# Turning normed tokens and slot rows by VectorE and transfers instead of TensorE, and a fixed engine for one copy

## The chip, the cores and the metric

The kernel runs on one core of a Trainium2 chip. The metric is the device time of one execution in microseconds, the median of several runs; lower is better. Profiled executions come with a trace of each engine: PE (TensorE's products), PEld (its weight loads), DVE (VectorE), ACT (ScalarE), POOL (GpSimd), and SPq, the queue on which SyncE issues transfers.

## The reference, cut to what matters

Two batches of 1024 tokens of 256 features pass through four residual steps, everything in float32:

```
x = x + L0_xattn(layernorm(x), ctx)       # 8 heads, softmax over 16 keys of the window
x = x + L0_ffn(layernorm(x))              # 8 groups, no nonlinearity between its two products
x = x + L1_xattn(layernorm(x), ctx, ctx)  # 16 heads, sigmoid instead of softmax
x = x + L1_ffn(layernorm(x))              # a mixture with 1024 slots

def L1_ffn(x):
    xn = rms_norm(x, gamma_x)
    se = rms_norm(slot_embeds, gamma_slot)
    logits = einsum('bsd,etd->bset', xn, se)
    dispatch = softmax(logits, over the tokens)
    slots = einsum('bsd,bset->betd', xn, dispatch)
    processed = gelu(slots @ w1) @ w2
    combine = softmax(logits, over the slots)
    return einsum('bnd,bsn->bsd', processed, combine)
```

The last step takes the larger part of the time. Below it is called the mixture, and the third step layer 1.

## The kernel before, in words

**Tiling.** The 2048 tokens are four quads of four tiles of 128 tokens; `xq[q]` holds a quad, tokens on the partitions, and is updated in place by each residual step. TensorE contracts over the partitions, so whatever is to be contracted over its features has to be turned first: features on the partitions, tokens along the row. The kernel before does that on TensorE, with a product against the identity, into a PSUM bank, and copies the bank to SBUF.

**Stages.** (1) The first attention runs per quad as `weigh` and `attend`. `attend` (L756) turns the attention weights on TensorE, copies them to `atT` (L762) and multiplies them with the folded values (L767). (2) The first feed-forward network folds its two weights per group g into one matrix (`product`, L522), and its biases into one row (`bias_rows`, mostly on VectorE at L553, then `bias`, L559); `norm_ff` and `feed_forward` use them per quad. (3) Layer 1 takes the quads in turn (L950). For each half c of the heads it makes scores (psg, L957), a Tanh on ScalarE (sg, L966) and the weighted values (poT, L996), whose eviction writes `oT` (L1003). Between scores and weighted values other work is put: at c = 0 the output product of the quad before (pf, L911), at c = 1 the queries of the next quad (pq, L897). (4) The mixture: `norm_tokens` (L154), `turn_tokens` (L175) and `logits` (L184) per token tile, then dispatch, `gather`, `hidden`, `processed` and `combine`.

**What is turned where.** `layernorm` (L482) of layer 1 writes `hn` and turns it by `transposed` (L120, eight turns of 128x128 on TensorE per quad, line L125, pt_a for layer 1, pt_f for the feed-forward network). `turn_tokens` turns the mixture's tokens in the same way (L180). `norm_slots` (L820) scales the 1024 slot rows by their own factor (squares L826, scaling L834), and `turn_slot_rows` turns a quarter of them at a time on TensorE (L842) while its eviction (L843) multiplies by the two gammas, which by then lie along the partitions. One tensor is already turned without TensorE: the mixture's combine weights `ec`. `turn` (L228) transposes blocks of 32x32 on VectorE (L236) into `tr`, and 16 transfers from SBUF to SBUF (L243) then put the blocks in their places.

**What sets the order.** A scheduler reorders the instructions of each engine at build time by program order and its own estimate of readiness; each engine then runs its queue strictly in the written order, and so does SyncE with its transfers. From L1012 on, ScalarE's order is as in the program. Operations written as `nc.any` are given to ScalarE or VectorE by the scheduler. Pools limit how many tiles of a tag are alive (`bufs`): a writer waits until the last reader of the tile that it replaces is done. Quad 1's `hn` takes the buffer that quad 0's turns on TensorE have read.

Of the kernel before, what the change touches and what calls it, by code (L numbers as in the profile page):

```python
# [9 lines left out]
FP = mybir.dt.float32  # L10
# [40 lines left out]
def tile_kernel(  # L51
# [9 lines left out]
    bo0: bass.AP,  # L61
    wff_in: bass.AP,
    b2: bass.AP,
    gammas: bass.AP,
    w1_in: bass.AP,
    slots_in: bass.AP,
# [25 lines left out]
    nc.gpsimd.memset(m_half, -0.5)  # L92
    xq = [const.tile([P, QT, D], FP, name=f"x{q}") for q in range(NQ)]

    gxs = const.tile([P, 2, DC], FP, name="gxs")
    gx, gs = gxs[:, 0, :], gxs[:, 1, :]
    ggx = const.tile([P, DC], FP, name="ggx")

    parity = const.tile([P, 2], FP, name="parity")
    nc.vector.tensor_reduce(  # L100
# [2 lines left out]
        AX.XY,  # L103
        ALU.add,
    )
    seT = const.tile([P, DC, NSLOT], FP, tag="seT", name="seT")

    def moments(xt, name):

# [10 lines left out]
    def transposed(src, dst, name, side=0):  # L120

        for c in range(DC):
            pt = bank(f"pt_{name}_{c}", side)
            for t in range(QT):
                nc.tensor.transpose(pt[:, ts(t, P)], src[:, t, ts(c, P)], ident)  # L125
            nc.any.tensor_copy(dst[:, c, :], pt)


    outr = out.rearrange("(q t p) d -> q p t d", t=QT, p=P)
# [43 lines left out]
        xhs[q] = xh  # L173

    def turn_tokens(q):  # L175
        xhT = pools["mw"].tile([P, DC, QN], FP, tag="xhT", name=f"xhT_{q}", bufs=2)
        for c in range(DC):
            pt = bank(f"pt_m_{q}_{c}", 1)
            for t in range(QT):
                nc.tensor.transpose(pt[:, ts(t, P)], xhs[q][:, t, ts(c, P)], ident)  # L180
            copy(c, xhT[:, c, :], pt)
        xhTs[q] = xhT

    def logits(b, s):  # L184

        q, t = b * QB + s // QT, s % QT
        if s == 0:
            zcs[b] = stat.tile([P, ST], FP, tag="zc", name=f"zc_{b}")
            rmaxs[b] = pools["md"].tile([P, NSLOT], FP, tag="rmax", name=f"rmax_{b}")
        lg = keep[b].tile([P, NSLOT], FP, tag=f"lg_{s}", name=f"lg_{b}_{s}")  # L190
        lgs[b][s] = lg
        nm = stat.tile([P, 2], FP, tag="nm", name=f"nm_{b}_{s}")
        for n in range(NSLOT // 512):
            pl = bank(f"pl_{b}_{s}_{n}", 0)
            for dc in range(DC):
                nc.tensor.matmul(  # L196
                    pl,
                    lhsT=xhTs[q][:, dc, ts(t, P)],
                    rhs=seT[:, dc, ts(n, 512)],
                    start=(dc == 0),  # L200
                    stop=(dc == DC - 1),
                )

            nc.vector.tensor_tensor_reduce(  # L204
                lg[:, ts(n, 512)], pl, zero.to_broadcast([P, 512]), -1.0,
                BIG if n == 0 else nm[:, 0:1], ALU.add, ALU.min, nm[:, n : n + 1],
            )

            rm = rmaxs[b][:, ts(n, 512)]
            if s == 1:  # L210
                nc.vector.scalar_tensor_tensor(
                    rm, lgs[b][0][:, ts(n, 512)], -1.0, pl, ALU.mult, ALU.max
                )
            elif s > 1:
                nc.vector.tensor_tensor(rm, rm, pl, ALU.max)
        if t == 0:

            ecs[q] = keep[b].tile([P, 2, QT, 512], FP, name=f"ec_{q}")
        nc.scalar.activation(  # L219
            ecs[q][:, :, t, :],  # L220
            lg.rearrange("p (h n) -> p h n", h=2),
            AF.Exp,
            bias=nm[:, 1:2],
            scale=-1.0,
            accum_out=zcs[b][:, s : s + 1],
        )
# [241 lines left out]
    with (  # L468
# [4 lines left out]
        wk1s, wv1s, wq1s, wo1s = (w1s[:, i] for i in range(4))  # L473
        se = w1p.tile([P, EC, D], FP, name="se")

        NCT, NPE = DC * 2 * B * NK, DC * NK
        fr = w1p.tile([P, NCT + NPE + NG * OC], FP, name="fr")
        ctxd = fr[:, 0:NCT].rearrange("p (c b e s) -> p c b e s", c=DC, b=B, e=2)
# [3 lines left out]
        def layernorm(xt, name, side=0):  # L482
            mv, rstd = moments(xt, name)
            hn = lnp.tile([P, QT, D], FP, tag="hn", name=f"hn_{name}")
            for t in range(QT):
                nc.vector.tensor_scalar(  # L486
                    hn[:, t, :], xt[:, t, :], mv[:, t, 0:1], rstd[:, t : t + 1],
                    ALU.subtract, ALU.mult,
                )
            hT = lnp.tile([P, DC, QN], FP, tag="hT", name=f"hT_{name}")  # L490
            transposed(hn, hT, name, side)
            return hT

        wide = ExitStack()
# [96 lines left out]
        def load_layer1():  # L591
            nc.sync.dma_start(out=w1s, in_=w1_in)
            nc.sync.dma_start(out=se, in_=slots_in)
            nc.sync.dma_start(out=gxs, in_=gammas)

        with tc.tile_pool(name="p0", bufs=1) as p0, tc.tile_pool(name="a0", bufs=2) as a0:

# [158 lines left out]
            def attend(q):  # L756
# [2 lines left out]
                for t in range(QT):  # L759
                    nc.tensor.transpose(pat[:, ts(t, P)], atf[:, ts(t, P)], ident)  # L760
                atT = a0.tile([P, QN], FP, tag="atT", name=f"atT_{q}")
                nc.any.tensor_copy(atT, pat)  # L762
                for i in range(2):
                    po = bank(f"po0_{q}_{i}")
                    for k in range(2):
# [49 lines left out]
        with (  # L815
# [4 lines left out]
            def norm_slots():  # L820
# [9 lines left out]
                nc.vector.tensor_scalar(sn, sn, RMS_EPS, None, ALU.max)  # L830
                nc.vector.reciprocal(sn, sn)
                nc.vector.tensor_scalar(sn, sn, float(D) ** 0.5, None, ALU.mult)
                for c in range(EC):
                    nc.vector.tensor_scalar(  # L834
                        se[:, c, :], se[:, c, :], sn[:, c : c + 1], None, ALU.mult
                    )
                nc.vector.tensor_tensor(ggx, gx, gs, ALU.mult)

            def turn_slot_rows(dc, h):
                pt = bank(f"pse_{dc}_{h}", 1)  # L840
                for c in range(4):
                    nc.tensor.transpose(pt[:, ts(c, P)], se[:, 4 * h + c, ts(dc, P)], ident)  # L842
                nc.vector.tensor_scalar(  # L843
                    seT[:, dc, ts(h, 512)], pt, ggx[:, dc : dc + 1], None, ALU.mult
                )

# [82 lines left out]
            for c in range(C1):  # L931
# [12 lines left out]
                None,  # L944
                ALU.mult,
            )
            queries(0)
            bias(7)
            work = ExitStack()
            for q in range(NQ):  # L950
                b = q * QN // S
                oTs[q] = a1.tile([P, C1, QN], FP, tag="oT", name=f"oT_{q}")
                for c in range(C1):
# [15 lines left out]
                    if c == 0:  # L969
                        if q == 0:  # L970
# [4 lines left out]
                            pools["mw"] = work.enter_context(  # L975
                                tc.tile_pool(name="mw", bufs=1, reuse_waits="tile")
                            )
                            norm_slots()
                        if q + 1 < NQ:
                            hTs[q + 1] = layernorm(xq[q + 1], f"a1_{q + 1}", 1)  # L980
                        if q > 0:
                            output(q - 1, (0, 1) if q + 1 < NQ else (0,))
                            turn_slot_rows(*divmod(q - 1, 2))
                        if q + 1 == NQ:
                            turn_tokens(0)
                    elif q + 1 < NQ:
                        queries(q + 1)
                        if q + 2 == NQ:
                            norm_tokens(0)
                            turn_slot_rows(1, 1)  # L990
                    else:
                        output(q - 1, (1,))
                        logits(0, 0)
# [21 lines left out]
    for u in range(1, B * ST + 2):  # L1015
        b, s = divmod(u, ST)
        if b < B:
            if s % QT == 1:
                q = u // QT + 1
                if q < NQ:  # L1020
                    norm_tokens(q)
            logits(b, s)
            if s % QT == 2:
                q = u // QT + 1
                if q < NQ:
                    turn_tokens(q)
        v = u - ST
        if v == 1:
            nc.vector.reciprocal(zcs[0], zcs[0])
# [113 lines left out]
```

## Time and profile before

| | |
|---|---|
| median of 3 runs | 461.45 us (461.29 to 461.98) |
| the profiled execution | 461.42 us, of which the trace's span is 459.6 us |
| granted TensorE clock | 1.00 throughout |
| first products of stage 1 and 2 end, layer 1's loop begins | about 123 us |
| first logits of the mixture | 170.0 us |
| last logits, gather begins | about 236 us |
| hidden and output of batch 0, gather of batch 1 begins | 347 us |
| VectorE's busy time in 66 to 108 us | 38.1 of 42 us |
| VectorE's busy time in 120 to 180 us | 35.2 of 60 us |
| ScalarE's busy time in the same 60 us | 24.7 us |
| transfers issued between 81 and 241 us | none |

A profile's group line reads: line, engine, operation, destination <- sources, count, then busy time and mean nanoseconds of one. A line of the waits names who waited for whom, the sum in us, how often and the longest. A line of the chain of work that ended last, or of a timeline, gives start, duration and what ran. Matrix products in float32 are recorded twice per instruction, turns once.

### The profile page before, as it was taken

What the parts mean: (1) busy time and instruction counts of PE and PEld (TensorE: products, weight loads), DVE (VectorE), ACT (ScalarE), POOL (GpSimd) and SP (SyncE); (2) the same over time, 40 slices, a digit from 0 to 9 for tenths busy, and PEclk for the clock granted to TensorE, in tenths of its full rate; (3) what the DMA queues carried; (4) which work ended last, traced back from release to release, by engine and by line L of the source; (5) the groups of instructions that cost most, each with busy time, mean ns of one, the idle gap of its engine ahead of it and who ended that gap; (6) DMA issues with size and microseconds to landing.
All of it is one profiled execution on the core that took longest, in us unless ns stands there. A gap on an engine that the chain in (4) does not pass through costs nothing.

```text
span 459.6 us, 5446 instructions
## 1 busy us (share of the span) xinstructions
PE 446.4 (97%) x2032; PEld 322.2 (70%) x2032; DVE 261.1 (57%) x623; ACT 110.8 (24%) x205; POOL 84.9 (18%) x84
## 2 busy tenths in 40 slices
PE   6999897999999999999999999999999999999997
PEld 5788795888645555445458854688888874488886
DVE  0487889897256677987776279611331539911111
ACT  1212331211344441342573306300000003410000
POOL 3011332325111101100878910000000000000000
PEclk9999999999999999999999999999999999999999
DMA  8994691500000000000007534140252040430011
GB/s 287 411 429 198 260 427 45 185 0 1 1 1 0 2 0 1 0 0 1 0 1 227 89 52 72 33 80 0 52 98 36 12 79 1 82 102 1 11 47 35
DMA packets 74381, 38.61 MB, mean 84 GB/s; under 512 B 68465, under 2 KB 70641, under 8 KB 72945
## 3 DMA queue, kind: packets, MB, share of 16 engines
q1 hardware_dynamic: 74354, 38.26, 27.4%
q8 instruction: 16, 0.26, 0.2%
q14 instruction: 11, 0.09, 0.1%
HBM read 27.76 MB, written 2.10 MB: 65 GB/s over the span
## 4 chain that ended last, share of the span: by engine, by line
PE 82%; DVE 6%; POOL 1%; issue 0%
PE psl L289 12%; PE pc L455 12%; PE pp L430 12%; PE pl L196 11%; PE pmh L364 11%; PE pmt L522 6%; PE pq L897 3%; PE pf L911 3%; PE po L580 2%; PE psg L957 2%; PE poT L996 2%; DVE b2z L553 1%; DVE hn_f L486 1%; PE po L767 1%; PE pt_a L125 1%; PE pb L273 1%
## 5 line engine op out<-in xcount | busy, mean ns | idle before, releaser
L522 PE MATMUL pmt<-wg 128*128 128x256 f32 x256 | 60.1, 393 | 3.8 <-DMA wg<-in_wff_dram 3.8
L289 PE MATMUL psl<-xh,lg 128*128 128x258 f32 x256 | 58.7, 381 | 0.0
L522 PEld LDWEIGHTS pmt<-wg 128*128 128x128 f32 x256 | 49.9, 198 | 11.4 <-DMA wg<-in_wff_dram 4.3
L196 PE MATMUL pl<-seT,xhT 128*128 128x512 f32 x128 | 56.1, 592 | 0.0
L455 PE MATMUL pc<-pr,ec 128*128 128x256 f32 x256 | 55.6, 379 | 0.0
L430 PE MATMUL pp<-ms,mh 128*128 128x256 f32 x256 | 55.6, 379 | 0.0
L430 PEld LDWEIGHTS pp<-ms,mh 128*128 128x128 f32 x256 | 48.6, 190 | 7.5 <-DVE mh L408 0.5
L455 PEld LDWEIGHTS pc<-pr,ec 128*128 128x128 f32 x256 | 48.6, 190 | 6.6
L289 PEld LDWEIGHTS psl<-xh,lg 128*128 128x128 f32 x256 | 47.4, 190 | 7.2 <-issue 0.5
L196 PEld LDWEIGHTS pl<-seT,xhT 128*128 128x128 f32 x128 | 24.1, 190 | 27.9 <-issue 26.3
L278 POOL TENSOR_TENSOR lg<-lg,mb 128x1024 f32<-128x1024 f32 x16 | 37.2, 2366 | 32.3 <-ACT mb L150 27.9
L462 DVE SCALAR_TENSOR_TENSOR x<-pc,zc,x 128x256 f32<-128x256 f32 x16 | 7.7, 484 | 42.3 <-PE pc L455 42.3
L442 DVE COPY pr<-pp 128x512 f32<-128x512 f32 x8 | 5.5, 692 | 45.5 <-PE pp L430 45.5
L219 ACT ACTIVATE ec<-lg,nm 128x1024 f32<-128x1024 f32 x16 | 18.4, 1148 | 41.6 <-DVE nm L204 41.6
L398 ACT COPY mh<-pmh 128x512 f32<-128x512 f32 x8 | 4.6, 572 | 89.6 <-PE pmh L364 89.6
L374 ACT ACTIVATE mh<-mh 128x512 f32<-128x512 f32 x32 | 19.0, 626 | 21.1 <-DVE mh L408 16.1
L364 PE MATMUL pmh<-slT,ms 128*128 128x512 f32 x48 | 24.0, 592 | 0.0
L553 DVE SCALAR_TENSOR_TENSOR b2z<-wg,fr,b2z 128x256 f32<-128x256 f32 x48 | 23.6, 494 | 0.3
L297 DVE RECIPROCAL rz<-psl 128x1 f32<-128x1 f32 x16 | 2.6, 164 | 32.7 <-PE psl L289 32.7
L966 ACT ACTIVATE sg<-psg 128x512 f32<-128x512 f32 x32 | 16.5, 603 | 18.0 <-PE psg L957 18.0
L236 DVE STREAM_TRANSPOSE tr<-ec 128x512 f32<-128x512 f32 x32 | 20.1, 679 | 0.0
L281 ACT ACTIVATE lg<-lg 128x1024 f32<-128x1024 f32 x16 | 16.5, 1049 | 12.2 <-POOL lg L278 12.2
(169 smaller groups left out, 585.9 us busy)
## 6 DMA issues: line engine op xcount, KB each, us to landing
wg<-in_wff_dram SPq DMA_DIRECT2D x6, 2048.0 KB, 12.4
ec<-tr SPq DMA_DIRECT2D x128, 64.0 KB, 2.1
xT<-in_xT_dram SPq DMA_DIRECT2D x4, 512.0 KB, 13.4
x<-in_x_dram SPq DMA_DIRECT2D x4, 512.0 KB, 14.9
wg<-in_wff_dram SPq DMA_DIRECT2D x2, 1024.0 KB, 11.3
ms<-in_m_dram SPq DMA_DIRECT2D x1, 2048.0 KB, 8.3
out_dram<-x SPq DMA_DIRECT2D x16, 128.0 KB, 1.8
wg<-in_wff_dram SPq DMA_DIRECT2D x3, 512.0 KB, 6.0
```

What stands on the lines that cost most here:

```text
L196: nc.tensor.matmul(pl, lhsT=xhTs[q][:, dc, ts(t, P)], rhs=seT[:, dc, ts(n, 512)], start=(dc == 0), stop=(dc == DC - 1),)
L219: nc.scalar.activation(ecs[q][:, :, t, :], lg.rearrange("p (h n) -> p h n", h=2), AF.Exp, bias=nm[:, 1:2], scale=-1.0, accum_out=zcs[b][:, ...
L236: nc.vector.transpose(tr[:, :, :, t, :].rearrange("p r c n -> p c r n"), half[:, t, :].rearrange("p (c r n) -> p c r n", c=EC // 2, r=R4),)
L278: nc.gpsimd.tensor_tensor(lgs[b][s], lgs[b][s], mbs[b], ALU.add)
L281: nc.scalar.activation(lgs[b][s], lgs[b][s], AF.Exp, scale=-1.0)
L289: nc.tensor.matmul(pz[:, 0:XW], lhsT=lgs[b][s][:, ts(c, P)], rhs=xhs[b * QB + s // QT][:, s % QT, :], start=(s == 0), stop=(s == ST - 1),)
L364: nc.tensor.matmul(to, lhsT=lefts[i][:, ts(j, P)], rhs=slTs[b][:, i, 0:512] if i < 2 else rights[b][i], start=True, stop=True,)
L374: nc.scalar.activation(h, h, AF.Gelu)
L430: nc.tensor.matmul(pp[:, ts(k, D)], lhsT=hss[b, g, fc // 2][:, fc % 2, ts(2 * c2 + k, P)], rhs=m12s[1][:, fc, :], start=(fc == 0), stop=(f ...
L455: nc.tensor.matmul(pc[:, 0:D], lhsT=turned[:, c // 4, c % 4, t, :], rhs=prs[b, c // 4][:, c % 4, :], start=(c == 0), stop=(c == EC - 1),)
L522: nc.tensor.matmul(pm[:, ts(hc, D)], lhsT=w1g[:, oc, ts(hc, P)], rhs=w2g[:, oc, :], start=(oc == 0 and hc == 0), stop=(oc == OC - 1 and hc ...
L553: nc.vector.scalar_tensor_tensor(acc, weights[g][1][:, oc, :], b1s[:, g, oc : oc + 1], acc, ALU.mult, ALU.add)
```

## The change

Six things are done together.

1. A function `turned` does what `turn` does for `ec`, for a tile of four times 128x256: four block transposes on VectorE into `tr`, then 16 transfers on SyncE.
2. Layer 1's quads 1 to 3 (not quad 0), all four quads of the mixture's tokens, and the slot rows in two halves are turned by it. The feed-forward network's norms stay on TensorE.
3. The norms are written earlier: quad 1's before layer 1's first queries, quad q + 2's during quad q; the mixture's quads 0 and 1 during layer 1's quads 1 and 2, and quads 2 and 3 at the first and third token tile of the logits. `hT` and `xhT` get three buffers instead of two.
4. The gammas can no longer be applied while slot rows are evicted, as there is no eviction. Both are loaded as rows on all partitions, multiplied by GpSimd, and GpSimd multiplies the slot rows by them; the scaling by the rows' own factors goes from VectorE to ScalarE.
5. `seT` is laid out by halves of slots.
6. The copy of `atT` is fixed to ScalarE.

```
+    def turned(src, dst, tr):
+        for t in range(QT):
+            nc.vector.transpose(
+                tr[:, :, :, t, :].rearrange("p r c n -> p c r n"),
+                src[:, t, 0:D].rearrange("p (c r n) -> p c r n", c=DC, r=R4),
+            )
+        to = dst.rearrange("p c (t i n) -> p (c t) i n", t=QT, i=R4)
+        for i in range(R4):
+            for r in range(R4):
+                nc.sync.dma_start(
+                    out=to[ts(r, SQ), :, i, :],
+                    in_=tr[ts(i, SQ), r].rearrange("p c t n -> p (c t) n"),
+                )
...
     def turn_tokens(q):
-        xhT = pools["mw"].tile([P, DC, QN], FP, tag="xhT", name=f"xhT_{q}", bufs=2)
-        for c in range(DC):
-            pt = bank(f"pt_m_{q}_{c}", 1)
-            for t in range(QT):
-                nc.tensor.transpose(pt[:, ts(t, P)], xhs[q][:, t, ts(c, P)], ident)
-            copy(c, xhT[:, c, :], pt)
+        xhT = pools["mw"].tile([P, DC, QN], FP, tag="xhT", name=f"xhT_{q}", bufs=3)
+        tr = pools["mw"].tile([P, R4, DC, QT, SQ], FP, tag="tr", name=f"tr_m_{q}", bufs=2)
+        turned(xhs[q], xhT, tr)
...
-            hT = lnp.tile([P, DC, QN], FP, tag="hT", name=f"hT_{name}")
-            transposed(hn, hT, name, side)
+            hT = lnp.tile([P, DC, QN], FP, tag="hT", name=f"hT_{name}", bufs=3)
+            if side is None:
+                tr = lnp.tile([P, R4, DC, QT, SQ], FP, tag="tr", name=f"tr_{name}")
+                turned(hn, hT, tr)
+            else:
+                transposed(hn, hT, name, side)
...
-            nc.sync.dma_start(out=gxs, in_=gammas)
+            nc.sync.dma_start(out=gx, in_=gx_in)
+            nc.sync.dma_start(out=ggb, in_=gammas.partition_broadcast(P))
...
-                nc.any.tensor_copy(atT, pat)
+                nc.scalar.copy(atT, pat)
...
+                gg = ggb[:, 0, :]
+                nc.gpsimd.tensor_tensor(gg, gg, ggb[:, 1, :], ALU.mult)
                 for c in range(EC):
-                    nc.vector.tensor_scalar(
-                        se[:, c, :], se[:, c, :], sn[:, c : c + 1], None, ALU.mult
-                    )
-                nc.vector.tensor_tensor(ggx, gx, gs, ALU.mult)
+                    nc.scalar.activation(
+                        se[:, c, :], se[:, c, :], AF.Copy, scale=sn[:, c : c + 1]
+                    )
+                for h in range(2):
+                    sh = se[:, ts(h, QT), :]
+                    nc.gpsimd.tensor_tensor(
+                        sh, sh, gg.unsqueeze(1).to_broadcast([P, QT, D]), ALU.mult
+                    )
-            def turn_slot_rows(dc, h):
...
+            def turn_slot_rows(h):
+                tr = lnp.tile([P, R4, DC, QT, SQ], FP, tag="tr", name=f"tr_se_{h}")
+                turned(se[:, ts(h, QT), :], seT[:, h], tr)
...
+            hTs[1] = layernorm(xq[1], "a1_1", None)
             queries(0)
             bias(7)
+            norm_slots()
+            turn_slot_rows(0)
...
-                            norm_slots()
-                        if q + 1 < NQ:
-                            hTs[q + 1] = layernorm(xq[q + 1], f"a1_{q + 1}", 1)
+                        if q + 2 < NQ:
+                            hTs[q + 2] = layernorm(xq[q + 2], f"a1_{q + 2}", None)
                         if q > 0:
                             output(q - 1, (0, 1) if q + 1 < NQ else (0,))
-                            turn_slot_rows(*divmod(q - 1, 2))
-                        if q + 1 == NQ:
-                            turn_tokens(0)
                     elif q + 1 < NQ:
                         queries(q + 1)
-                        if q + 2 == NQ:
-                            norm_tokens(0)
-                            turn_slot_rows(1, 1)
+                        if 0 < q:
+                            norm_tokens(q - 1)
+                            turn_tokens(q - 1)
+                        if q == 0:
+                            turn_slot_rows(1)
...
-            if s % QT == 1:
-                q = u // QT + 1
-                if q < NQ:
-                    norm_tokens(q)
+            if u in (1, 3):
+                norm_tokens(QB + u // 2)
+                turn_tokens(QB + u // 2)
             logits(b, s)
-            if s % QT == 2:
-                q = u // QT + 1
-                if q < NQ:
-                    turn_tokens(q)
```

## The prediction

> **What bounds the kernel now.** I read the page's shares first, then TensorE's own waits, then the chain that ended last.
>
> ```profile
> PE 446.4 (97%) x2032; PEld 322.2 (70%) x2032; DVE 261.1 (57%) x623; ACT 110.8 (24%) x205; POOL 84.9 (18%) x84
> ```
>
> ```profile
> PE pmt L522 <- DMA wg<-in_wff_dram: 3.8, 1, 3.8
> PE po L767 <- DVE atT L762: 3.4, 1, 3.4
> PE pt_f L125 <- DVE e L741: 1.2, 1, 1.2
> PE pwk L686 <- ACT vblk L675: 1.0, 1, 1.0
> PE po L767 <- ACT atT L762: 0.7, 1, 0.7
> ```
>
> TensorE is the bound: 97% busy, and its waits sum to 10.1 us in 459.6. They all lie before 73 us; from there to the last product it never starves. So an instruction taken off TensorE after 73 us is worth its pitch on TensorE, if the data that it made still arrives in time. The chain gives the pitch (an instruction's mean of 270 ns overlaps its neighbours):
>
> ```profile
> 131.36 3.63 PE pq L897 x8
> 134.99 1.00 PE poT L996 x8
> 135.98 1.07 PE psg L957 x8
> 137.05 1.02 PE pt_a L125 x8
> 138.08 3.46 PE pf L911 x16
> 141.53 0.44 PE pse L842 x4
> 141.97 0.99 PE poT L996 x8
> 142.97 1.07 PE psg L957 x8
> ```
>
> Eight turns of normed tokens take 0.87 to 1.02 us, four turns of slot rows 0.44. One quad of layer 1 is pq to pq, 12.7 us.
>
> The other resource that matters is the sync queue, since the mixture's weights are already turned in the new way. The answer for the tile tr (minimum, median, maximum ns):
>
> ```profile
> L243 SPq DMA_DIRECT2D ec<-tr x128: 585/627/1613, 245.5 to 401.4; - x128
> L236 DVE STREAM_TRANSPOSE tr<-ec x32: 668/670/712, 242.5 to 390.7; 128x512 f32<-128x512 f32 x32
> DMA to landing us min/median/max: 2.1/2.1/5.0
> ```
>
> Sixteen transfers follow one another at 0.63 us though each lands 2.1 us later: the issue is what is serial. Between 81 and 241 us that queue issues nothing in this kernel.
>
> **What is removed.** Off TensorE go the turns of layer 1's quads 1 to 3 (0.87 + 1.02 + 1.02 = 2.9 us in the chain), of four slot-row parts (4 x 0.44 = 1.8) and of four mixture quads (4 x 0.87 = 3.5): 72 turns, **8.2 us**. All lie after 110 us, where TensorE is the bound.
>
> **The copy of atT.** VectorE's timeline in the one attend that waits:
>
> ```profile
> 70.35 1.00 DVE L553 SCALAR_TENSOR_TENSOR b2z<-wg,fr,b2z 128x256 f32<-128x256 f32 x2
> 71.26 0.15 DVE L837 TENSOR_TENSOR ggx<-gxs 128x2 f32<-128x2 f32 x1
> 71.33 0.68 DVE L739 TENSOR_REDUCE mx<-psc 128x32 f32<-128x512 f32 x1
> 71.94 0.68 DVE L762 COPY atT<-pat 128x512 f32<-128x512 f32 x1
> ```
>
> The turned weights stood ready at 68.0; VectorE copied them at 71.9, behind bias rows. ScalarE is idle from 66.5 to 73.3 and takes 0.58 us, so it is done near 68.7, before TensorE has finished the six products that it does meanwhile (69.3). The wait of **3.4 us** goes. What is late next? attend(3)'s weights, at L751 at 76.7 to 77.4, were used at 81.4; TensorE will ask at 78.0, and VectorE has one copy of 0.6 us less before them: no wait. Weight group 7 is issued at 80.3 and asked for at 107: covered.
>
> Together 11.5 us: with nothing late, 459.6 - 11.5 + 1.8 outside the span = 449.9.
>
> **What is added, engine by engine.**
> - VectorE: nine groups (quads 1 to 3, two slot halves, four mixture quads) of four turns of 128x256. L236 is 0.62 us back to back at twice the size, a 128x256 operation 0.34 to 0.40: 1.5 us a group, 13 in all. It loses one of the two copies of most turned tiles (four xhT, two hT_a at 0.69), four seT evictions (3.0), eight slot scalings (2.4) and one atT: 10.2. Net +3 us over 130 us, in which it is idle some 40 us: nothing by itself. Its order matters: below.
> - ScalarE: eight scalings by the row factor instead of VectorE's, taken as 0.4 us like the squares (0.42): 3.2 us near 97 us, where it idles for ten. Behind them waits the copy of product 6 at 101.7, with 3 us to spare; without that cover they would cost up to 3 us. It loses about 4.6 us of evictions.
> - GpSimd: two products of 128x1024 at 2.37 us (row L278) and a small one, 5.3 us. It idles from 97.8 to 104.0; rstd and the bias sums queue behind. A VectorE normalization beside a GpSimd product can be held up (hn_f: 406 ns median, 1361 at most, beside L574 at 65.0), here at most 2.4 us, and TensorE asks for those norms over 5 us later: zero.
> - The gammas as rows: 256 KB more to load at 50 us, at the 430 GB/s of that stretch 0.6 us before weight group 6, which has 20 us of slack: zero. The layout of seT keeps runs of 512: zero.
> - The norms written earlier: the trace has mixture quad 1's statistics at 153 us, though its call stands after layer 1, so the scheduler hoists them already: zero. Moved with them are their 16 transfers each, counted next.
> - SyncE: 9 x 16 = 144 transfers of 32 KB (256 runs of 128 bytes) on an empty queue. No row has this size. Plain loads issue in 0.33 us, L243 with 512 such runs in 0.63; a line between 128 and 512 runs gives 0.43. I take 0.55, nearer to the row with the same pattern; 0.43 to 0.63 is the range.
>
> Here a rule speaks against the change. The Trainium skill, "VectorE: DVE Perf Modes", section "Rules for kernel authors", says to turn 128x128 on TensorE where PSUM will do; and "DMA: Bandwidth & Descriptors", under the same section title, that transfers under 64 KB are mostly overhead. If the 2.1 us of a transfer were paid in a row, six groups would take 202 us where there are 59, some 140 us slower. L243's row decides: at 0.63 they overlap. On TensorE's side the rule forgets that here TensorE is the bound: its 0.9 us per quad are dearer than 10 us of an idle queue.
>
> **The deadlines.** TensorE's new times, the chain less 3.4 and less each removed turn: quad 1 asked for at 127.1, quad 2 at 138.3, quad 3 at 149.5 (pitch now 11.2 us), mixture quad 0 and both slot halves at 161.4. Slot rows can be turned from 102 us (their factors are there at 96.9, then 3 to 5 us of scaling); quad 1's norm only after its buffer is free, near 107.5, so transferred from 112. Through 161.4 six groups must pass, 96 transfers.
> - At 0.55: 102 + 52.8 + 2.1 = 156.9, in time. Quad 1 behind one slot half is there at 121.7, behind both at 130.5, 3.4 late. The trace doesn't show which order the scheduler will write; I take half, **1.7 us**.
> - Shorter covers: oT's eviction (0.75 + 0.15) had 2.1 us of psg and pt_a before pf, now 1.07, so any VectorE operation in front shows: 0.3 us in each of three quads. In the last quad Tanh (2.06) is covered by 2.01 of pf: 0.4. **1.3 us**, between 0 and 3.
>
> Sum: 459.6 - 8.2 - 3.4 + 1.7 + 1.3 = 451.0; outside the span 1.8, so 452.8 on the execution of 461.42. The median of the runs is 461.45: **453 us**.
>
> **The rivals.**
> - Full cover (12%): pace 0.43, no waits: 449.9. For it: 11 us of lead for each norm. Against it: the in-order oT.
> - A slow queue (16%): 0.63 and both slot halves first. Quad 1 is there at 102 + 30.2 + 2.1 = 134.3, 7.2 late: 449.9 + 7.2 + 1.3 = 458.4. For it: the only row of such transfers.
> - Slower (16%): the slot rows are not turned early; the queue starts at 112 with quad 1. At 0.63, 112 + 60.5 + 2.1 = 174.6, so the first logits wait 13.2 us: 449.9 + 13.2 + 1.3 = 464.4. It decides from a start after 109 at 0.63, or a pace above 0.70 from 102. VectorE's in-order turns, waiting for a buffer tr that transfers still read, are the way there. Against it: the slot scalings ran at 98 to 101 before, and at 0.55 even 112 costs only 5.5 us.
> - Nothing comes of it (6%): VectorE's bias rows bound the stretch to 110 us, so the 3.4 come back as a later wait, and the queue takes the rest. Against: the last bias row is done at 100.9, and its product runs at 106.8. About 461.5.
>
> **The numbers.** My own case has 50%, 451 to 455.5. A measurement here tells 0.2%, 0.9 us, from no change. Faster by more 78% (50 + 12 + 16), within 6%, slower 16%. The range leaves out most of the slower case: 449.3 to 462.2.
>
> **What would show it.** Pitch of pq to pq: 11.2 us, otherwise a wait of pq on DMA names the queue. No wait of L767 on VectorE. Issue time of the new transfers: 0.43 to 0.63; above 0.70 I am wrong in sign. First logits near 161 to 164 us. After that the two kernels should run alike, 2.6 us apart more by the three later mixture quads. Slot rows issued before 105 us speak for my case, after 112 for the slower one. A wait for norms behind GpSimd's products, or of evictions behind a VectorE turn that waits for tr, would show a cost that I set at zero.

## The result and the profile after

The changed kernel takes 474.06 us in the median of four runs (473.63 to 475.35), against 461.52 us (461.29 to 461.98) for the kernel before beside it: a ratio of 1.0275, with a 95% interval of 1.0252 to 1.0298. It is **12.5 us slower**; 8.5 us less were forecast. The profiled execution took 473.7 us, its span is 471.9 us. The part of the page with the shares:

```profile
PE 441.9 (94%) x1960; PEld 315.0 (67%) x1960; DVE 266.4 (56%) x638; ACT 111.8 (24%) x207; POOL 90.4 (19%) x87
```

72 instructions have left TensorE, as meant, and its busy time fell by 4.5 us although part of the rest ran at a lower clock. The span grew nonetheless, so what was added is idle time of TensorE. Its waits (in total, times, longest, in us):

```profile
PE pq L921 <- DMA hT_a<-tr_a: 16.3, 3, 7.7
...
PE pmt L543 <- issue: 2.3, 1, 2.3
...
PE pb L288 <- DVE dg L274: 0.7, 1, 0.7
```

The wait of 3.4 us for VectorE's copy of atT is gone. Two large ones are new: the queries wait three times for the transferred norms, 16.3 us in all, and product 7 (pmt) waits 2.3 us for something that the profile cannot name. Small ones join them, such as the 0.7 us for dg in the mixture. TensorE's timeline of the stretch, with the idle time before a row and its releaser in brackets:

```profile
109.49 7.14 PE L543 MATMUL pmt<-wg 128*128 128x256 f32 x32 [2.32 <-issue]
...
130.05 3.67 PE L921 MATMUL pq<-hT_a,w1s 128*128 128x512 f32 x8 [1.00 <-DMA hT_a<-tr_a]
...
149.20 5.78 PE L921 MATMUL pq<-hT_a,w1s 128*128 128x512 f32 x8 [7.69 <-DMA hT_a<-tr_a]
```

The same eight products take 3.67 us at 130 and 5.78 at 149, after the long wait. The stretches' table (busy time of each engine, then the granted clock) says why: TensorE was given 0.72 of its clock there, and 0.75 around the third wait.

```profile
144.00:156.00 12.00, 6.80 (x20) 2.49 (x20) 5.02 (x18) 1.17 (x2) 1.85 (x2) 0.72 0.34 50
...
168.00:180.00 12.00, 9.59 (x35) 4.14 (x38) 2.15 (x6) 3.23 (x6) 0.00 (x0) 0.75 0.32 48
```

A table of milestones on TensorE's two timelines gives the balance, in us:

| start of | before | after | difference |
|---|---|---|---|
| second product of stage 2, ahead of all that was changed | 28.21 | 26.71 | -1.5 |
| quad 0's turns, pt_a | 109.84 | 106.13 | -3.7 |
| product 7 | 110.92 | 109.49 | -1.4 |
| quad 1's queries | 131.29 | 130.05 | -1.2 |
| quad 2's queries | 143.97 | 149.20 | +5.2 |
| quad 3's queries | 156.65 | 170.41 | +13.8 |
| first logits | 170.00 | 183.90 | +13.9 |
| end of the span | 459.6 | 471.9 | +12.3 |

The first row is chance: the program's very first product took 10.03 us in the one traced execution and 8.61 in the other, and nothing of the change lies before it. So at product 7 the changed kernel has in truth gained nothing, and all of the loss arises between 130 and 171 us, at the two waits of 7.7 us. What follows returns 1.6 us, mainly the turns of three token quads.

**The queue behind it.** SyncE's timeline:

```profile
114.36 3.35 SPq L141 DMA_DIRECT2D seT<-tr_se  x5
117.82 10.41 SPq L141 DMA_DIRECT2D hT_a<-tr_a  x16
128.28 8.50 SPq L141 DMA_DIRECT2D seT<-tr_se  x11
136.96 10.78 SPq L141 DMA_DIRECT2D hT_a<-tr_a  x16
147.84 10.54 SPq L141 DMA_DIRECT2D seT<-tr_se  x16
158.55 10.40 SPq L141 DMA_DIRECT2D hT_a<-tr_a  x16
169.05 1.24 SPq L141 DMA_DIRECT2D xhT<-tr_m  x2
```

It starts at 114.4 and issues with hardly a pause to past 169: the first 80 transfers in 54.6 us, 0.68 us each (a set of 16 takes 10.4 us, 0.65 each; the first of all took 1.96). Each quad's 16 transfers stand behind slot rows that nobody needs before the logits. Quad 2's begin at 137.0 and end at 147.7, and its queries start 1.5 us after that; they could have been used at 141.5. The answer for the transfers' line (minimum, median, maximum ns):

```profile
L141 SPq DMA_DIRECT2D hT_a<-tr_a x48: 585/609/620, 117.8 to 168.3; - x48
L141 SPq DMA_DIRECT2D seT<-tr_se x32: 586/609/1957, 114.4 to 157.8; - x32
...
DMA to landing us min/median/max: 1.9/2.0/3.9
```

An issue takes 0.61 us at half the bytes of L243, whose issue took 0.63. VectorE's timeline shows why nothing was issued before 114:

```profile
96.42 2.23 DVE L574 SCALAR_TENSOR_TENSOR b2z<-wg,fr,b2z 128x256 f32<-128x256 f32 x1
...
99.18 1.98 DVE L574 SCALAR_TENSOR_TENSOR b2z<-wg,fr,b2z 128x256 f32<-128x256 f32 x1
...
108.28 1.11 DVE L886 TENSOR_SCALAR kblk<-pk,parity 128x128 f32<-128x128 f32 x4
...
109.46 0.82 DVE L909 COPY vblk<-pv 64x256 f32<-64x256 f32 x2
110.32 1.38 DVE L503 TENSOR_SCALAR hn_a<-x,mv_a,rstd_a 128x256 f32<-128x256 f32 x4
111.61 1.41 DVE L134 STREAM_TRANSPOSE tr_a<-hn_a 128x256 f32<-128x256 f32 x4
112.96 1.38 DVE L134 STREAM_TRANSPOSE tr_se<-se 128x256 f32<-128x256 f32 x4
```

The scaled slot rows are ready on GpSimd at 100.9, but VectorE's order has their turns behind the whole of quad 1's norm, at 112.96. Two bias rows took 2.23 and 1.98 us where such a row is 0.48 alone: they run beside GpSimd's two slot products (95.84 to 100.88).

### The profile page after: what moved, and what is told of

Its sections match the earlier page's. It is cut to its first block, busy times and chain, and to the rows that moved or that the text cites. A ratio compares the mean times of both kernels' runs of the same rounds, so it can differ in the third digit from the quotient of the medians.

```text
span 471.9 us, 5540 instructions
## 1 busy us (share of the span) xinstructions
PE 441.9 (94%) x1960; PEld 315.0 (67%) x1960; DVE 266.4 (56%) x638; ACT 111.8 (24%) x207; POOL 90.4 (19%) x87
## 4 chain that ended last, share of the span: by engine, by line
PE 73%; DVE 6%; SPq 6%; issue 2%; DMA 1%; ACT 1%; POOL 1%; ACTq 0%
PE pc L470 12%; PE pp L445 12%; PE psl L304 11%; PE pl L211 11%; PE pmh L379 10%; PE pmt L543 6%; SPq L141 6%; PE pq L921 3%; PE po L601 1%; PE pf L935 1%; DMA hT_a<-tr_a 1%; DVE b2z L574 1%; DVE hn_f L503 1%; PE psg L984 1%; PE poT L1021 1%
## 5 line engine op out<-in xcount | busy, mean ns | idle before, releaser
L543 PE MATMUL pmt<-wg 128*128 128x256 f32 x256 | 58.7, 387 | 6.0 <-DMA wg<-in_wff_dram 3.7
L921 PE MATMUL pq<-hT_a,w1s 128*128 128x512 f32 x32 | 18.5, 732 | 16.3 <-DMA hT_a<-tr_a 16.3
L574 DVE SCALAR_TENSOR_TENSOR b2z<-wg,fr,b2z 128x256 f32<-128x256 f32 x48 | 26.3, 549 | 0.3
L921 PEld LDWEIGHTS pq<-hT_a,w1s 128*128 128x128 f32 x32 | 7.2, 237 | 26.9 <-issue 24.9
## 6 DMA issues: line engine op xcount, KB each, us to landing
wg<-in_wff_dram SPq DMA_DIRECT2D x6, 2048.0 KB, 13.8
```

Source lines behind the costliest of these rows:

```text
L543: nc.tensor.matmul(pm[:, ts(hc, D)], lhsT=w1g[:, oc, ts(hc, P)], rhs=w2g[:, oc, :], start=(oc == 0 and hc == 0), stop=(oc == OC - 1 and hc ...
L574: nc.vector.scalar_tensor_tensor(acc, weights[g][1][:, oc, :], b1s[:, g, oc : oc + 1], acc, ALU.mult, ALU.add)
L921: nc.tensor.matmul(pq, lhsT=wq1s[:, dc, ts(c, P)], rhs=hTs[q][:, dc, :], start=(dc == 0), stop=(dc == DC - 1),)
```

## The experiments

My theory Q: the queue. It starts late, one issue costs 0.61 us whatever is in it, and the slot rows stand in front of the norms. The rival V: VectorE in its written order is too full, and would give the waits back elsewhere even with a free queue. Ratios are to the kernel before, run beside them, with a 95% interval.

**1. Slot rows back on TensorE.** Everything else is as changed; 32 transfers less stand in the queue.

```
             def turn_slot_rows(h):
-                tr = lnp.tile([P, R4, DC, QT, SQ], FP, tag="tr", name=f"tr_se_{h}")
-                turned(se[:, ts(h, QT), :], seT[:, h], tr)
+                for dc in range(DC):
+                    pt = bank(f"pse_{dc}_{h}", 1)
+                    for c in range(4):
+                        nc.tensor.transpose(pt[:, ts(c, P)], se[:, 4 * h + c, ts(dc, P)], ident)
+                    nc.vector.tensor_copy(seT[:, h, dc, :], pt)
```

> The changed kernel, but the slot rows are turned on TensorE again (their norms stay on ScalarE and GpSimd), so 32 of the 80 transfers before layer 1's last queries leave the sync queue. Theory Q (the sync queue's issue, 0.65 us a transfer, is what layer 1 waits for): the 16.3 us of waits of pq fall to 1 us or less and the products after them run at full clock again (4.3 us), against 1.8 us for 16 turns: 474 - 16.3 - 4.3 + 1.8 = 455 us. Theory V (VectorE's strict order and its longer work delay the quads): the turns of hn still stand at the same places, the waits stay over 10 us and the time over 466 us.

Measured 459.86 us, ratio 0.9955 (0.9940 to 0.9969). Its waits:

```profile
...
PE pmt L543 <- issue: 2.3, 1, 2.3
PE pf L938 <- DVE oT L1031: 1.7, 2, 0.9
```

No query waits for a transfer any more. So the 16.3 us belong to the slot rows' transfers, and 14.2 us of the time with them. It is 5 us above my number. The 2.3 us at product 7 are in both kernels; what is new is a stretch of 3.4 us at half clock behind them (some 1.7 us), waits for oT's eviction (1.7 us), and, by chance, a first product of the program that took 9.61 us in this execution and 8.61 in that of the changed kernel (about 1 us).

**2. Half of these transfers from ScalarE's queue** (those with odd r, for layer 1 and the slot rows).

```
-                nc.sync.dma_start(
+                (nc.scalar if r % 2 and two else nc.sync).dma_start(
```

> The changed kernel, but for layer 1's quads and the slot rows every second transfer is issued from ScalarE's queue. Same transfers, same bytes, half of them on each queue. Theory Q: the issue is what is serial, so the waits of pq go and the time falls to 453 to 456 us, unless ScalarE's Tanh is held up behind its 40 issues (0.6 us each, 24 us in all). If the transfers themselves (their 128-byte runs, their landing) were the limit, two queues would change nothing: 472 us or more. Theory V: over 466 us.

Measured 465.01 us, ratio 1.0081 (1.0055 to 1.0107). The queue's waits are gone here too, with the same number of transfers and bytes: what was short was the issuing, not the transport. My number was missed by over 9 us. An issue takes ScalarE 0.62 us as it takes SyncE, and two things follow. The copies of the queries moved to VectorE, behind its other work, and the Tanh stands behind transfers, as the expectation had feared:

```profile
PE psg L984 <- DVE qT L928: 2.4, 2, 2.0
...
143.36 4.82 ACTq L141 DMA_DIRECT2D hT_a<-tr_a  x7
148.29 2.06 ACT L993 ACTIVATE sg<-psg 128x512 f32<-128x512 f32 x4 [4.50 <-DMA hT_a<-tr_a]
```

The scores of that Tanh were done at 146.0. From quad 1's queries to the first logits TensorE takes 42.5 us, where the changed kernel takes 34.7 without its waits for transfers and the half clock behind them: 7.8 us more, of which 2.4 are listed as waits for qT and 1.1 for oT; the rest lies in the weighted values' products behind the late Tanh. The half clock after product 7 adds 1.7 us and the program's first product, by chance, 1.4.

**3. The kernel before with only atT fixed to ScalarE.**

```
-                nc.any.tensor_copy(atT, pat)
+                nc.scalar.copy(atT, pat)
```

> The kernel before with atT copied by ScalarE and nothing else. By the prediction's step the wait of 3.4 us goes: 458.1 us. By the trace after the change, product 7 then waits for a bank that VectorE empties at 109.4 (2.3 us), and two products of attend wait 0.9 us for VectorE: the gain is 0.2 to 1.2 us, 460.3 to 461.3 us.

Measured 462.05 us, ratio 1.0002 (0.9992 to 1.0011): nothing. In its waits the 3.4 us are replaced by this:

```profile
PE pmt L522 <- issue: 2.7, 1, 2.7
```

TensorE stands still from 107.6 to 110.3, when it starts product 7. VectorE's timeline ends one row at that moment:

```profile
109.10 1.11 DVE L862 TENSOR_SCALAR kblk<-pk,parity 128x128 f32<-128x128 f32 x4
```

kblk is what empties the PSUM bank of pk. In the kernel before, the same two rows read:

```profile
109.70 1.11 DVE L862 TENSOR_SCALAR kblk<-pk,parity 128x128 f32<-128x128 f32 x4
...
110.92 7.14 PE L522 MATMUL pmt<-wg 128*128 128x256 f32 x32
```

There too product 7 starts 0.1 us after kblk's end (110.81), only that TensorE has quad 0's turns to do until then and no wait shows. VectorE reaches kblk only 0.6 us earlier than before, so most of the 3.4 us gained at 70 us end at 110. Experiment 5 tests that reading.

**4. The kernel before with only the mixture's tokens turned in the new way**, their norms written as early as in the change, atT as before.

```
     def turn_tokens(q):
...
+        tr = pools["mw"].tile([P, R4, DC, QT, SQ], FP, tag="tr", name=f"tr_m_{q}", bufs=2)
+        turned(xhs[q], xhT, tr)
...
+                        if 0 < q:
+                            norm_tokens(q - 1)
+                            turn_tokens(q - 1)
```

> The kernel before with only the mixture's tokens turned by VectorE and transfers (norms at the places of the change); layer 1 and slot rows as before. Theory Q: 64 transfers from 148 us on, with deadlines 14 us apart or more, 10.4 us a quad: the first one must be in place at 168 us and is, none waits, and the 3.5 us of 32 turns are gained: 458 us. Theory V: VectorE is full between 180 and 204 us and gets 0.8 us more a quad there, so evictions of the logits come late: 460 us or more.

Measured 465.78 us, ratio 1.0086 (1.0071 to 1.0101): with 3.5 us of turns less and no wait for a transfer, 4 us slower. Its waits:

```profile
PE po L783 <- DVE atT L778: 3.4, 1, 3.4
PE pt_a L125 <- DVE hn_a L502: 2.8, 2, 2.5
...
PE pf L927 <- DVE oT L1019: 1.1, 1, 1.1
```

and on VectorE's timeline what stands between the first tile of quad 3's norm and the other three:

```profile
150.10 0.41 DVE L502 TENSOR_SCALAR hn_a<-x,mv_a,rstd_a 128x256 f32<-128x256 f32 x1 [1.24 <-POOL rstd_a L117]
150.43 1.38 DVE L188 TENSOR_SCALAR xh<-x,mv_m,f 128x256 f32<-128x256 f32 x4
151.72 1.41 DVE L135 STREAM_TRANSPOSE tr_m<-xh 128x256 f32<-128x256 f32 x4
153.06 1.01 DVE L502 TENSOR_SCALAR hn_a<-x,mv_a,rstd_a 128x256 f32<-128x256 f32 x3
```

V's number came, though not at the place that it had named (evictions of the logits): tokens that nobody needs for another 24 us stand in front of a norm that TensorE waits for. The sum: -3.5 for the turns, +2.8, +1.1 and +0.7 (dg) for new waits, and about +3.4 for two stretches at half clock, one of them behind the wait for atT: +4.5. Measured are +3.8 against all executions of the kernel before, and +4.4 against those of them that show no such stretch (461.39, see TensorE's clock below).

**5. Experiment 3 and kblk by ScalarE too.** In the next kernels this edit is called "kblk by ScalarE".

```
-                    nc.vector.tensor_scalar(
+                    nc.scalar.activation(
                         kblk[:, c, :, e, :],
                         pk[:, ts(c, P)].rearrange("p (b s) -> p b s", b=B),
-                        parity[:, e : e + 1],
-                        None,
-                        ALU.mult,
+                        AF.Copy,
+                        scale=parity[:, e : e + 1],
                     )
```

> The kernel before with atT copied by ScalarE and the four kblk operations, which empty the bank that product 7 wants, on ScalarE too. If VectorE's backlog up to 110 us is what takes the gain of atT back, at that bank, then with kblk off VectorE product 7 starts with no wait and the time is 458 to 459 us. If product 7 waits for something else, 461 to 462 us.

Measured 457.44 us, ratio 0.9905 (0.9888 to 0.9921). No wait of pmt on "issue" is left, the clock is 1.00, and the 3.4 us of atT arrive: product 7 starts 79.5 us after the second product of stage 2, in place of 82.7. The bank was the cause. The 4.4 us measured are one more than that, and not by this edit: 19 of the 31 executions of the kernel before beside it show a stretch at half clock (against the other 12, 461.46 us, the gain is 4.0), and the program's first product was 0.9 us shorter in the traced execution than in that of before.

**6. The changed kernel with its slot rows turned earlier**, ahead of kblk.

```
+            norm_slots()
+            turn_slot_rows(0)
+            turn_slot_rows(1)
             kblk = a1c.tile([P, C1, B, 2, NK], FP, name="kblk")
...
             bias(7)
-            norm_slots()
-            turn_slot_rows(0)
...
-                        if q == 0:
-                            turn_slot_rows(1)
```

> The changed kernel with the slot rows' norms and both turned halves written ahead of layer 1's keys, so that their 32 transfers can use the queue before quad 1's norm is there. Same 144 transfers. Theory Q with the start as the cause: slot rows from about 103 us, quad 1 behind them at 103 + 48 x 0.65 + 2 = 136 us, asked for at 129: one wait of 6 to 7 us, quads 2 and 3 in time; 474 - 10 - 3 (half clock) = 460 to 462 us. If the start is not it: 470 us or more.

Measured 462.75 us, ratio 1.0023 (1.0013 to 1.0032). The queue's first transfer is issued at 100.5, all 32 slot transfers are past at 121.9, and no query waits. That does not show that the early start is enough, for TensorE itself came late: quad 1 was asked for at 136.4, in the changed kernel at 129. Its transfers, issued from 122.0, should have landed near 134.5 (16 at 0.65 and 2.0 to land, an estimate), over 5 us too late for 129. What held TensorE up is that the same turns now stand before the eviction of quad 3's feed-forward norm:

```profile
PE po L601 <- DVE hT_f L126: 6.8, 1, 6.8
```

and the clock is 0.50 from about 103 to 113. VectorE reached that copy at 106.4, after 2.9 us of slot turns and bias rows that had been pushed back (two of them took from 94.7 to 97.9, beside GpSimd's slot product). In the kernel before and in the changed one both copies of this norm are ScalarE's; here the scheduler gave one of them to VectorE, while ScalarE did nothing from 100.2 to 113.6.

**7. One set of 16 transfers of 64 KB for all slot rows**, where the changed kernel has two of 16 of 32 KB; the call stands where the first half's stood, and xhT has two buffers in place of three.

```
-            def turn_slot_rows(h):
-                tr = lnp.tile([P, R4, DC, QT, SQ], FP, tag="tr", name=f"tr_se_{h}")
-                turned(se[:, ts(h, QT), :], seT[:, h], tr)
+            def turn_slot_rows():
+                tr = a1c.tile([P, R4, 2, DC, QT, SQ], FP, name="tr_se")
...
+                to = seT.rearrange("p h c (t i n) -> p (h c t) i n", t=QT, i=R4)
+                for i in range(R4):
+                    for r in range(R4):
+                        nc.sync.dma_start(
+                            out=to[ts(r, SQ), :, i, :],
+                            in_=tr[ts(i, SQ), r].rearrange("p h c t n -> p (h c t) n"),
+                        )
```

> The changed kernel with both halves of the slot rows in one group of 16 transfers of 64 KB instead of 32 of 32 KB, at the place of the first half (two xhT buffers instead of three, for space). Same bytes, 16 issues fewer. Theory Q (the price is per issue, not per byte): quad 1 at 114.4 + 28 x 0.65 + 2 = 134.6, 5.5 late, quad 2 some 2 late, quad 3 in time: 461 to 463 us. If bytes or runs set the pace, the waits stay: 472 us or more.

Measured 462.58 us, ratio 1.0016 (1.0007 to 1.0025). The answer for the tile:

```profile
L878 SPq DMA_DIRECT2D seT<-tr_se x16: 608/627/741, 106.4 to 131.1; - x16
```

Twice the bytes cost 3% more time to issue: for this pattern the price is per transfer. No query waits. The time was as expected, but by luck, on a detour that I had not foreseen: the eight turns went before kblk in VectorE's order, at 103.6, the four operations of hn_f behind them took 4.24 us in place of 1.37 (beside GpSimd's sums of x), and product 7 waits 5.3 us for its bank in place of 2.3.

**8. Experiment 1 with kblk by ScalarE.**

> The changed kernel with slot rows turned on TensorE (as in e1) and kblk on ScalarE. The 2.3 us before product 7 and the half clock behind it (1.7 us) go, the rest is e1's: 459.9 - 4.0 = 455.9 us. If VectorE's backlog (bias rows behind GpSimd's product of the slot rows) only meets TensorE at the next bank instead: 458 us or more.

Measured 455.36 us, ratio 0.9872 (0.9857 to 0.9886). The wait at product 7 is gone, no query waits for a transfer, though quad 1 is asked for as early as in the changed kernel (at 128.7 and 129.0), and the clock is 1.00 up to the last 5 us. This is the change as it was made, less the slot rows in the queue and less the one bank.

**9. Slot rows as in 7 but ahead of kblk as in 6, kblk by ScalarE, and the tokens' norms written after oT's eviction.** It was meant as the best one with everything turned.

```
-                        if 0 < q:
-                            norm_tokens(q - 1)
-                            turn_tokens(q - 1)
...
                         oTs[q][:, c, :], po, 0.5, vsum[:, c, b : b + 1], ALU.mult, ALU.add
                     )
+                    if c == 1 and 0 < q < NQ - 1:
+                        norm_tokens(q - 1)
+                        turn_tokens(q - 1)
```

> The changed kernel with the slot rows in one group of 64 KB transfers, written ahead of layer 1's keys, with kblk on ScalarE, and with the mixture's norms written after oT's eviction. Theory Q: slot rows in place by 116 us, no quad waits, product 7 neither: 8.2 us of turns and about 3 us of the atT wait are gained, less some 2 us at oT and at the largest values' diagonal: 452 to 454 us, faster than both kernels. Theory V: VectorE's order still delays quads, 458 us or more.

Measured 462.94 us, ratio 1.0025 (1.0017 to 1.0033), 9 us above the upper end of my number. Its first wait is that of experiment 6, 6.8 us for hT_f, with the clock down behind it, and oT is waited for 1.7 us as in experiment 1, so the tokens' new place did not help. Theory Q alone did not give a fast kernel: where the slot turns were early enough for the queue, they were in VectorE's way. Whether they need be is open: hT_f's copy was not fixed to ScalarE, as kblk's was.

**10. Slot rows wholly as before (VectorE's scaling, TensorE's turns), layer 1 and the tokens turned in the new way, atT and kblk by ScalarE.**

> The changed kernel without what it does to the slot rows (their norms on VectorE, their turns on TensorE, both gammas in the eviction, at the places of the kernel before), and with kblk on ScalarE: GpSimd's two products of 128x1024 and 32 transfers are gone. From e5 (457.4): 2.9 + 3.5 us of turns off TensorE, less some 1.7 us of pf waiting for oT: 452 to 454 us. If the norms written ahead crowd VectorE before 110 us as the early slot rows did: 457 us or more.

Measured 455.93 us, ratio 0.9882 (0.9867 to 0.9896), about 2 us more than expected. The wait for oT is there:

```profile
PE pf L931 <- DVE oT L1024: 2.0, 2, 1.1
```

**11. Experiment 7 with kblk by ScalarE.**

> e7 (the changed kernel, slot rows in one group of 64 KB transfers at their place) with kblk on ScalarE. e7's wait of 5.3 us before product 7 goes with the half clock behind it (1.7), but the queue then is asked 5 us sooner: quad 1 asked for near 128, there near 134 as in the sum for e7: 1 to 6 us come back as a wait of pq on transfers. 456 to 461 us; without the queue's deadline 455.5.

Measured 458.17 us, ratio 0.9928 (0.9914 to 0.9943). TensorE now comes earlier, and the queue is felt again:

```profile
PE pq L932 <- DMA hT_a<-tr_a: 2.6, 1, 2.6
```

**12. The kernel before with only layer 1's quads 1 to 3 turned in the new way, atT and kblk by ScalarE**; their norms are written as early as in the change, tokens and slot rows are as before. The core of the diff to before, beside atT and kblk:

```
-            hT = lnp.tile([P, DC, QN], FP, tag="hT", name=f"hT_{name}")
-            transposed(hn, hT, name, side)
+            hT = lnp.tile([P, DC, QN], FP, tag="hT", name=f"hT_{name}", bufs=3)
+            if side is None:
+                tr = lnp.tile([P, R4, DC, QT, SQ], FP, tag="tr", name=f"tr_{name}")
+                turned(hn, hT, tr)
+            else:
+                transposed(hn, hT, name, side)
```

> e10 with the mixture's tokens turned on TensorE as before, so only layer 1's quads 1 to 3 go by VectorE and transfers: 48 transfers from 114 us, 31 us of queue. 457.4 - 2.9 = 454.5 us if nothing waits, and no oT wait behind VectorE's token turns. If e10 is faster by 2 us or more the tokens' part is worth its transfers; if they are equal, VectorE's waits eat it.

Measured 455.33 us, ratio 0.9869 (0.9852 to 0.9885), with experiment 8 the fastest. All of its waits:

```profile
PE pmt L546 <- DMA wg<-in_wff_dram: 3.8, 1, 3.8
PE pt_f L126 <- DVE e L765: 1.2, 1, 1.2
PE pwk L710 <- ACT vblk L699: 1.0, 1, 1.0
PE po L791 <- ACT atT L786: 0.7, 1, 0.7
PE po L791 <- DVE x L611: 0.5, 2, 0.3
```

Against experiment 5 it gains some 2 us (457.44 to 455.33), of the 2.9 that these turns cost TensorE. Against experiment 10 it lacks the tokens' 3.5 us and is not slower: of what the tokens' turns save on TensorE, waits for oT (2.0) and dg (0.7) take most back.

## Why the prediction was wrong, step by step

**The deadlines: this step failed.** It put the queue's start at 102 us, "Slot rows can be turned from 102 us (their factors are there at 96.9, then 3 to 5 us of scaling)", and a transfer every 0.55 us. The rows were indeed there at 100.9. The step asked when the data would be ready, and not where in VectorE's written order the turn would stand. VectorE turned them at 113.0, behind the bias rows, kblk, vblk and quad 1's norm, and the queue began at 114.4. The pitch was 0.68. By the step's own rule the 80 transfers up to quad 3's last would have been issued by 146.0; they were at 169.0, and of these 23 us 12.4 are the start and 10.6 the pitch. The slot rows' transfers came between the quads', so each quad met its own delay. The term "1.7 us" for the queue was 16.3 us. Experiments 1 and 8 show it by taking the slot rows out, experiment 2 by issuing from two queues: none has such a wait. That an early start alone would have done is not shown (experiment 6). Nor was another order tried, the quads first; by an estimate it would only have moved the wait: 96 transfers at 0.65 from 114.4, and 2.0 to land, end at 178.8, while TensorE without its waits and half clock would ask for the logits at 163.7.

My rival "Slower" had the mechanism (the slot rows are not turned early, the pace is 0.63) and the point from which it decides (a start after 109), but not the order. It let quad 1 go first and all be late at the logits: 13.2 us there. The queue's surplus was paid instead by quads 2 and 3, and the logits waited for no transfer. I argued against it with "the slot scalings ran at 98 to 101 before"; that is the row of an operation, not of the turn written after it.

**The pace.** I interpolated between plain loads and L243, by the number of runs. Within this pattern that number and the bytes hardly matter: 0.609 us for 256 runs and 32 KB, 0.627 for 512 and 64 KB. What makes a plain load's issue shorter (0.33) stays open. L243, the only row of the same pattern, gave the answer, and I leaned away from it.

**TensorE's clock: a term that the sum lacked.** In the profile before, the clock was 1.00 throughout, and I counted a wait at its own length. After, the two waits of 7.7 us each brought a stretch of 6.8 us at half clock. The products behind them took 5.78 and 5.41 us in place of 3.67: 3.9 us more. The Trainium skill, "TensorE: Matmul & The Clock Gate", section "What's actually happening", tells of a free-running window of about 3.4 us after which an idle array is given half its clock; the stretches seen here are one, two or three times 3.41 us, which agrees. It asks for an idle window; here waits of 2.3 to 2.7 us (experiments 1 to 4) brought such a stretch, and the 2.3 us of the changed kernel itself didn't. The same 3.4 us for atT brought none in the trace of before and one in that of experiment 4. One kernel can go either way as well: of the 15 executions of the kernel before beside experiments 1 to 4, four show a clock of 1.00 and take 461.4 us in the median; eleven show 0.996, which is what one stretch makes of the mean (1.7 of 460 us lost), and take 462.3. The measurement decides: between 2.3 and 3.4 us of waiting it can go either way.

**The copy of atT: right in place, wrong in worth.** The wait went, though 0.9 us came back at the same products, as waits for VectorE's additions to x. "What is late next?" was answered with attend(3) and weight group 7, and the bank that kblk empties was missed: 2.3 of the 3.4 us came back there, in experiment 3 all of it. My rival "Nothing comes of it" had said that VectorE bounds the stretch to 110 us. I dismissed it by the last bias row, at 100.9; the row that counted was kblk, near 110. Experiments 3 and 5 settle this.

**GpSimd's products: not zero for VectorE.** I looked for the norms that they might hold up. They held up the bias rows: the group of 48 went from 23.6 to 26.3 us, 2.7 us of VectorE's time, in the stretch where VectorE is the bound. The Trainium skill, "SBUF — State Buffer", section "Who interferes with whom", says it: an operation of VectorE with two inputs in SBUF contends with one of GpSimd that reads SBUF, and b2z has two. The hold-up shown is 1.5 to 1.8 us per bias row, against the "at most 2.4" that I allowed for a norm and then set to zero. Little of it reached TensorE: counted from the second product of stage 2, product 7 starts at 82.8 us in the changed kernel and at 82.3 in experiment 3, which has no such GpSimd products.

**VectorE's net +3 us: "nothing by itself. Its order matters".** The size of a turn was right (a group of four takes 1.38 to 1.42 us, 1.5 was said), and the second sentence should have been worked out. Each version with slot rows or tokens turned in a new place, and no queue wait, lost time to VectorE's order: hn_a (2.8), hT_f (6.8), the bank (5.3), qT (2.4), oT (1.7 to 2.0). Experiment 12, with layer 1 alone, did not.

**What was right.** The turns taken off TensorE are worth their pitch where nothing is late: after the first logits the changed kernel gains, and experiment 12 gets some 2 of 2.9 us. The tokens' transfers are in time in every run. With the queue and the bank mended, experiment 8, the prediction's sum holds within 2.4 us: 461.45 - 8.2 + 1.8 (slot rows stay) - 3.4 + 1.3 = 452.95, measured 455.36. Its waits sum to 10.0 us, where the 10.1 of before less 3.4 are 6.7: oT was waited for 1.7 us, where the "shorter covers" were put at 1.3, and the sum had nothing for the 0.9 of the additions to x and the 0.7 of dg.

**The balance of the changed kernel**, from the two traces: -1.5 by chance at the program's first product; +0.1 from there to product 7, where atT's 3.4 us are used up by the additions to x, the bank and small delays; +16.3 for the queue, +3.9 for the clock, +0.7 for dg. That is +19.5, and the span's +12.3 leaves -7.2 for the turns, of the 8.2 forecast: from query to query, without waits and half clock, the changed kernel takes 11.5 us, not 11.2. Why a removed turn brings a little less than its pitch stays open.

## What to carry to other kernels

When work is moved to an engine or a queue that looks idle, ask where its instruction will stand in that engine's written order, not when its data are ready, and list each queue's entries in order with their deadlines: an urgent transfer behind 16 that aren't urgent is 10 us late. Where a wait on the path is removed, follow the engine that caused it to its next result that the path needs; if that one does not come earlier, the gain is gone there. Count a wait of some 2.3 us or more on TensorE with up to 1.7 us on top for each 3.4 us stretch at half clock that the work behind it may run in. And before a difference of 1 us between two traces is explained, check that they are level where nothing was changed yet.

## What the runs showed that I had not expected

- One issue of a strided SBUF-to-SBUF transfer took 0.61 us at 32 KB and 0.63 at 64 KB, on SyncE as on ScalarE (0.62), and on ScalarE it takes its time from the copies.
- A wait of 6.8 us on TensorE came with half clock from about 103 to 113 us (experiments 6 and 9).
- The program's first product took from 8.6 to 10.0 us in the traces, with the same instructions.
- A bias row of 0.48 us took 2.23 us beside a GpSimd product (changed kernel).
- A wait that the profile calls "issue" was a PSUM bank not yet emptied, 2.3 to 5.3 us (changed kernel, experiments 1 to 3 and 7); with kblk on ScalarE it was gone (5, 8 to 12).
